# Bias of a layer's outputs from VectorE to TensorE for four tiles, and a routing product one slot later

## The chip, the cores and the metric

The kernel runs on one core of a Trainium2 chip (trn2), in one launch. The metric is the device time in microseconds, the median of several executions. Engines are named as in the profile: PE is TensorE's matmul, PEld its weight load, DVE VectorE, ACT ScalarE, POOL GpSimd, SP SyncE, which issues most DMAs.

## The reference, cut to what matters

Input x has 2 batches of 2048 tokens of 256 values, float32 throughout. Everything is dense except the last layer, where each token uses one of 8 matrices:

```python
xn  = layernorm(layernorm(x)) * ln_gamma + ln_beta
q, k, v = heads(xn @ w_q.T), heads(xn @ w_k.T), heads(xn @ w_v.T)      # 4 heads of 64
sim = rmsnorm(q, q_gamma) * 64**-0.5 @ rmsnorm(k, k_gamma).T
y   = softmax(sim) @ v            # heads side by side again
y   = y @ w_o.T + b_o             # the bias that the change moves
x2  = x + layernorm(y)
h   = layernorm(x2)
e   = argmax(h @ gate_w.T)        # one of 8 experts for each token
out = x2 + layernorm(h + h @ expert_w[e].T)
```

## The kernel before

**Attention.** A batch has 16 tiles of 128 tokens. The attention of both batches is 256 steps `(b, qb, c, kc)`: four blocks of 512 queries, two pairs of heads, 16 tiles of keys. Two steps make a slot; there are 128 slots. Within a slot the instructions are issued in this order: the scores `s` of the next slot on PE (L1071) with their exponentials `p` on ACT (L1079); the additions of this slot's `p` to the row sums `acc` on DVE (L1112, L1114); then `between(now)`, which lets every waiting side job do its next piece; then the weighted sums `po` of this slot on PE (L1123). The order on every engine is fixed by this program order, and each engine works through its own queue in order. The scores have two PSUM buffers (`ps_s`), the exponentials five SBUF buffers (`p`), `po` one, and all side jobs share three PSUM buffers (`ps_m`). A `p` buffer is free when its addition on DVE and its weighted sum on PE are done.

**Side jobs** are Python generators in a queue with due slots; each `yield later(...)` or bare `yield` ends the piece of one slot. `project` makes the queries, keys and values. `block_sums` normalises a finished block. `tokens` takes one tile of 128 tokens through the output product `py` (L817), the bias `y` (L832), the first layernorm (`norm`, statistics on DVE at L387 and L389, the root on POOL at L383), the residual `x2` (L843) and the scores of the experts (L851).

**Routing.** Batch 0 is group A (16 tiles), the first 12 tiles of batch 1 are group B, and the last four tiles are computed against all experts after the attention. When the last tile of a group has its scores, `choose_all` (L585 to L593) picks the experts, and the generator `order` sorts the group by expert in three pieces: a rank product on PE (L603, L604) with some two dozen small DVE instructions (`count` to `pos`, L613 to L652); a second DVE piece (`sl` to `inrow`, L655 to L686); after one piece with nothing in it the source product `src` on PE (L696), 16 matmuls with 23 columns for A and 12 with 19 for B, and its copy on DVE (L703). Every float32 matmul is two records in the profile.

The last piece of `order` also queues what follows: one `places` job per tile of places (23 for A, 19 for B), which gathers the rows with an indirect DMA on POOL (L722), loads the expert's matrix through SP into a ring (L736), turns and multiplies them on PE (`pt_g` L744, `pe` L754) and normalises; and one `collect` job per tile of the group (16 for A), which gathers the result on POOL (L792), reads `x2` through SP (L800), adds on DVE (L804) and stores through SP (L808). One job starts per slot, beginning with the slot after the source product; the `collect` jobs of A so run up to the last slots of the attention. Their tile `fg` has two buffers: the gather of a `collect` waits for the store of the one two before. After the last slot, `finish()` orders what is left with planned costs: the places of B, the last four tiles, and the collects of B.

Of the kernel before, what the change touches and what calls it, by code (L numbers as in the profile page):

```python
# [9 lines left out]
F32 = mybir.dt.float32  # L10
# [3 lines left out]
ALU = mybir.AluOpType  # L14
# [11 lines left out]
def kernel(  # L26
# [16 lines left out]
    nc = tc.nc  # L43
    P = 128
# [4 lines left out]
    NCH = D // P  # L49
# [4 lines left out]
    QT4 = KB // P  # L54
# [121 lines left out]
    DG = D + E  # L176
# [4 lines left out]
    bias_o = const.tile([P, DG], F32, tag="bias_o", name="bias_o")  # L181
# [100 lines left out]
    def bounded_path():  # L282
# [23 lines left out]
        wk = path.enter_context(tc.tile_pool(name="wk", bufs=2))  # L306
# [8 lines left out]
        allones = route.tile([P, P], F32, tag="allones", name="allones")  # L315
# [37 lines left out]
        def ps_m(name):  # L353
            return psum.tile([P, KB], F32, tag="ps_m", name=name, bufs=3)
# [242 lines left out]
        def order(gr):  # L597
# [43 lines left out]
            start = small.tile([P, E], F32, tag="start", name=f"start{n}")  # L641
# [49 lines left out]
                )  # L691
            yield
            yield
            ps = ps_m(f"src{n}")
            for t in range(T):
                nc.tensor.matmul(  # L696
# [3 lines left out]
                    start=(t == 0),  # L700
                    stop=(t == T - 1),
# [109 lines left out]
        def tokens(bt, qb, j, oTs, gr):  # L811


            tt = bt.b * NT + qb * QT4 + j
            py = ps_m(f"py{tt}")[:, :DG]
            for c, oT in enumerate(oTs):
                nc.tensor.matmul(  # L817
                    py,
                    oT[:, bass.ts(j, P)],
                    woT[:, c, :],  # L820
                    start=(c == 0),
                    stop=(c == NCH - 1),
                )
            yield then("DVE", 1.1)
            if gr:
                y = wk.tile([P, DG], F32, tag="y", name=f"y{tt}", bufs=3)
                xr = wk.tile([P, D], F32, tag="xr", name=f"xr{tt}")
            else:
                kept = wk.tile([P, HP, KB], F32, tag="p", name=f"kept{tt}", bufs=5)
                x2n, last = kept[:, 0, :D], kept[:, 0, D:]  # L830
                y, xr = kept[:, 1, KB - DG :], last
            nc.vector.tensor_tensor(y, py, bias_o, ALU.add)  # L832
            nc.sync.dma_start(out=xr, in_=x_f[tt * P : (tt + 1) * P, :])
            if gr:
                away = gr.away[:, tt - gr.first : tt - gr.first + 1]
# [18 lines left out]
            if not gr:  # L854
                pick = choose(small, score, tt)
            else:
                gr.met += 1
                if gr.met == gr.T:
                    choose_all(gr)
                    queue.append((now + 1 if gr is groups[0] else now, order(gr)))  # L860
                    queue.sort(key=lambda q: q[0])
# [22 lines left out]
            f = None  # L884
            EB = KB // D
            for e in range(E):
                if e % (HP * EB) == 0:
# [3 lines left out]
                    for r in range(HP):  # L891
                        for c in range(NCH):
# [6 lines left out]
                                start=(c == 0),  # L899
                                stop=(c == NCH - 1),  # L900
# [12 lines left out]
                f = z  # L913
# [61 lines left out]
        def finish():  # L975
# [3 lines left out]
            while queue or running:  # L979
                best = None  # L980
                for rank, g in enumerate(running + [g for _, g in queue]):
                    step = nexts.get(g) or opening.get(g) or Next("", 0.0)
                    if any(have[k] < step.take.count(k) for k in step.take):
                        continue
                    since = gates[g]() if g in gates else 0.0
                    if since is None:
                        continue
                    at = max(ready.get(g, 0.0), since, clear.get(step.engine, 0.0))
                    order = order_of.get(g, 0) if step.order < 0 else step.order
                    key = (at, order, rank)  # L990
                    if best is None or key < best[0]:
                        best = key, g, step
                (at, *_), g, step = best
                if g not in running:
                    queue[:] = [q for q in queue if q[1] is not g]
                    running.append(g)
                gates.pop(g, None)
                opening.pop(g, None)
                clock = end = at + step.cost
                clear[step.engine] = end if step.engine else 0.0  # L1000
                for k in step.take:
                    have[k] -= 1
                step = next(g, running)
                settle(g, step)
                if step is running:
                    running.remove(g)
                else:
                    ready[g] = end + (step.wait if step else 0.0)
# [4 lines left out]
        def opens(g, step, order, gate=None):  # L1013


            opening[g], order_of[g] = step, order
            if gate:
                gates[g] = gate
            return g
# [12 lines left out]
        groups = []  # L1032
# [107 lines left out]
        for g in range(len(steps) // PAIR):  # L1140
# [14 lines left out]
            b, qb, c, kc = steps[mine[-1]]  # L1155
            if kc == NT - 1:
                oT = wk.tile([P, KB], F32, tag="oT", name=f"oT{g}", bufs=4)
                nc.scalar.copy(oT, po)
                w = opens(block_sums(g, acc, oT), Next("PE", 1.0, take="m"), 0)
                queue.append((now, w))  # L1160
                oTs.append(oT)
                if c == NCH - 1:
                    tt = b * NT + qb * QT4
                    gr = next((g for g in groups if g.first <= tt < g.first + g.T), None)
                    last = gr and tt + QT4 == gr.first + gr.T
                    gap = (2 if gr is groups[0] else 1) if last else 4 if following else 1
                    for j in range(QT4):
                        w = tokens(batches[b], qb, j, oTs, gr)
                        end = (len(steps) // PAIR - 1, j)
                        opens(w, Next("PE", 0.5, take="m"), 0, lambda end=end: normed.get(end))  # L1170
                        queue.append((now + 2 + gap * j, w))
                    oTs = []
                queue.sort(key=lambda q: q[0])
# [381 lines left out]
```

## Time and profile before

| | |
|---|---|
| median of 3 executions | 804.57 us (802.62 to 805.9) |
| profiled execution: its own time | 796.33 us |
| profiled execution: span | 794.6 us |
| PE busy | 760.0 us, 96% |
| DVE busy | 607.9 us, 77% |
| ACT busy | 459.6 us, 58% |
| POOL busy | 323.9 us, 41% |
| mean granted TensorE clock | 0.982 |
| source product A starts | 460.6 us |
| rank product B starts | 678.4 us |
| last scores of the attention start | 711.4 us |

The profiled execution lies 8.2 us below the median of the others; 1.7 us of its own time lie around the span. Times such as "460.6 us" count from the start of the span. Lines of a timeline read: start, duration, engine, line, operation, output and inputs, count, and in brackets the idle time of the engine just before and what ended it.

### The profile page before, as it was taken

To read this page: it belongs to the slowest core of one execution; us is meant where nothing else is said; L and a number is where in the kernel's file an instruction comes from. 1 tells how busy PE (TensorE), PEld (TensorE's weight loads), DVE (VectorE), ACT (ScalarE), POOL (GpSimd) and SP (SyncE) were. 2 spreads that over 40 slices of the span, in tenths; PEclk is the share of its full clock that TensorE was granted. 3 is DMA by queue.
4 is the path that set the end of the run, shared out by engine and by line. 5 is a ranking of instruction groups with operands and counts; after the bars stand their busy time and mean duration, and the time that the engine had idled before them with its cause. 6 is when DMAs were issued, how large, how long until landed. Compare 5 with 4: busy or idle time off the path is not lost.

```text
span 794.6 us, 10249 instructions
## 1 busy us (share of the span) xinstructions
PE 760.0 (96%) x3169; PEld 320.3 (40%) x3169; DVE 607.9 (77%) x1239; ACT 459.6 (58%) x725; POOL 323.9 (41%) x349
## 2 busy tenths in 40 slices
PE   7999999999999999999999989999999999898794
PEld 5555433433343334333333343444444333335452
DVE  3666567598886877887888986777786889996767
ACT  3766765656565566556556525566656555445861
POOL 4644311133342523432325121757663455335324
PEclk9999999999999999999999979999999999899998
DMA  4100121210110000000221040443421243358336
GB/s 129 55 27 26 41 80 40 67 34 19 35 34 7 21 21 20 21 21 20 73 81 47 27 132 14 127 132 110 112 66 34 80 120 99 124 155 255 90 114 188
DMA packets 48149, 57.57 MB, mean 72 GB/s; under 512 B 5868, under 2 KB 39416, under 8 KB 48088
## 3 DMA queue, kind: packets, MB, share of 16 engines
q1 hardware_dynamic: 41528, 44.65, 17.8%
q0 software_dynamic: 3568, 9.32, 4.7%
q10 hardware_dynamic: 2992, 2.88, 1.3%
q8 instruction: 27, 0.44, 0.3%
q14 instruction: 34, 0.28, 0.1%
HBM read 37.69 MB, written 19.14 MB: 72 GB/s over the span
## 4 chain that ended last, share of the span: by engine, by line
PE 85%; DVE 8%; ACT 3%; issue 2%; POOL 2%; DMA 1%; POOLq 0%; DVEq 0%; ACTq 0%
PE s L1071 28%; PE po L1123 27%; PE pqk L464 7%; PE pv L473 4%; PE py L817 3%; PE peA L754 3%; PE pe L893 2%; PE pt_qk L501 2%; PE sm L1087 2%; DVE acc L1114 2%; PE pt_x L451 1%; PE peB L754 1%; DVE acc L1099 1%; PE srcA L696 1%; PE pt_gA L744 1%
## 5 line engine op out<-in xcount | busy, mean ns | idle before, releaser
L1079 ACT ACTIVATE p<-s,nbound 128x1024 f32<-128x1024 f32 x256 | 271.4, 1110 | 232.2 <-PE s L1071 224.5
L1114 DVE TENSOR_TENSOR acc<-acc,p 128x1024 f32<-128x1024 f32 x224 | 273.8, 1222 | 37.0 <-ACT p L1079 25.5
L1071 PE MATMUL s<-QT,KT 64*128 64x512 f32 x1024 | 256.5, 619 | 0.4 <-ACT p L1079 0.4
L1123 PE MATMUL po<-p,V 128*64 128x512 f32 x1024 | 251.6, 613 | 0.0
L1071 PEld LDWEIGHTS s<-QT,KT 64*128 64x128 f32 x1024 | 89.0, 188 | 164.6 <-issue 96.1
L1123 PEld LDWEIGHTS po<-p,V 128*64 128x64 f32 x1024 | 64.1, 137 | 129.8 <-issue 127.3
L383 POOL TENSOR_TENSOR rs_z<-rs_t,mhalf 128x1 f32<-128x1 f32 x28 | 36.8, 1316 | 123.3 <-DVE rs_t L382 123.2
L383 POOL TENSOR_TENSOR rn<-rs_t,mhalf 128x8 f32<-128x8 f32 x32 | 58.6, 1831 | 69.3 <-DVE rs_t L382 69.3
L464 PE MATMUL pqk<-wqkT,xnT 128*128 128x512 f32 x128 | 62.4, 611 | 0.6 <-ACT xnT L455 0.6
L383 POOL TENSOR_TENSOR roots<-rs_t,mhalf 128x1 f32<-128x1 f32 x32 | 23.9, 747 | 93.3 <-DVE rs_t L382 93.1
L1099 DVE RECIPROCAL acc<-acc 128x128 f32<-128x128 f32 x60 | 56.7, 945 | 0.0
L383 POOL TENSOR_TENSOR rs_y<-rs_t,mhalf 128x1 f32<-128x1 f32 x28 | 33.7, 1204 | 35.4 <-DVE rs_t L382 32.8
L832 DVE TENSOR_TENSOR y<-py,bias_o 128x264 f32<-128x264 f32 x28 | 12.0, 430 | 41.8 <-PE py L817 41.8
L722 POOL DMA_INDIRECT rows<-x2nA,srcA x23 | 28.9, 1257 | 30.1 <-DMA ring<-weTd 24.7
L817 PE MATMUL py<-woT,oT 128*128 128x264 f32 x128 | 35.7, 402 | 3.6 <-ACT xTB L749 2.3
L792 POOL DMA_INDIRECT fgA<-fnA,posA x16 | 18.2, 1136 | 44.8 <-DMA out_dram<-fgA 10.3
L473 PE MATMUL pv<-wvT,xnT 128*128 128x264 f32 x128 | 33.7, 386 | 0.0
L487 DVE TENSOR_REDUCE ss<-sq 128x8 f32<-128x512 f32 x32 | 21.8, 680 | 14.9 <-ACT sq L484 14.9
L473 PEld LDWEIGHTS pv<-wvT,xnT 128*128 128x128 f32 x128 | 24.5, 191 | 17.8 <-issue 10.4
L817 PEld LDWEIGHTS py<-woT,oT 128*128 128x128 f32 x128 | 22.0, 189 | 18.9 <-issue 12.1
L464 PEld LDWEIGHTS pqk<-wqkT,xnT 128*128 128x128 f32 x128 | 22.3, 195 | 17.7 <-issue 16.6
L481 ACT COPY qk<-pqk 128x512 f32<-128x512 f32 x32 | 18.7, 585 | 17.6 <-PE pqk L464 17.4
(270 smaller groups left out, 882.1 us busy)
## 6 DMA issues: line engine op xcount, KB each, us to landing
ring<-weTd SPq DMA_DIRECT2D x34, 256.0 KB, 2.9
x<-in_L_attn_x_dram SPq DMA_DIRECT2D x8, 512.0 KB, 3.9
xr<-in_L_attn_x_dram SPq DMA_DIRECT2D x28, 128.0 KB, 2.3
fnA<-fA SPq DMA_DIRECT2D x23, 128.0 KB, 2.5
we_raw<-in_L_ffn_expert_w_dram ACTq DMA_DIRECT2D x8, 256.0 KB, 2.7
weTd<-weT SPq DMA_DIRECT2D x8, 256.0 KB, 2.0
x2A<-x SPq DMA_DIRECT2D x16, 128.0 KB, 1.7
fgA<-x2A SPq DMA_DIRECT2D x16, 128.0 KB, 2.0
```

The lines of the kernel that those rows point to most:

```text
L383: nc.gpsimd.tensor_tensor(dst, t[:, :n], mhalf[:, :n], ALU.pow)
L464: nc.tensor.matmul(pqk, xnT[:, c, :], wqkT[:, c, :, :].rearrange("p a d -> p (a d)"), start=(c == 0), stop=(c == NCH - 1),)
L473: nc.tensor.matmul(pv[:, :DG], xnT[:, c, :], wvT[:, c, :], start=(c == 0), stop=(c == NCH - 1),)
L487: nc.vector.tensor_reduce(ss, sq.rearrange("p (g d) -> p g d", d=DH), AX.X, ALU.add)
L722: nc.gpsimd.indirect_dma_start(out=xg, out_offset=None, in_=gr.x2n[:, :], in_offset=bass.IndirectOffsetOnAxis(ap=gr.src[:, j : j + 1], axi ...
L754: nc.tensor.matmul(pe, xT[:, c, :], w[:, c, :], start=(c == 0), stop=(c == NCH - 1))
L817: nc.tensor.matmul(py, oT[:, bass.ts(j, P)], woT[:, c, :], start=(c == 0), stop=(c == NCH - 1),)
L1071: nc.tensor.matmul(s[:, r, :], bt.KT[rows, c, bass.ts(kc, P)], bt.QT[qb][rows, c, :], start=True, stop=True,)
L1079: nc.scalar.activation(p, s, AF.Exp, bias=nbound)
L1099: nc.vector.reciprocal(acc[:, 0, cols], share[:, cols])
L1114: nc.vector.tensor_tensor(acc, acc, p, ALU.add)
L1123: nc.tensor.matmul(po[r * DH : (r + 1) * DH, :], batches[b].V[:, kc, h * DH : (h + 1) * DH], p[:, r, :], start=(kc == 0), stop=(kc == NT - 1),
```

## The change

For group B's last four tiles (24 to 27 of all 32) `tokens` no longer adds the bias on DVE. PE adds it with a third matmul in the same PSUM group: a row of ones (one row, 128 columns) times the bias row (264 columns). The tile `y` is then the PSUM tile `py` itself, and the statistics, the residual and the experts' scores of those tiles read PSUM. In `order`, group A gets one more empty piece ahead of its source product.

```diff
@@ order
             yield
             yield
+            if gr is groups[0]:
+                yield
             ps = ps_m(f"src{n}")
@@ tokens
             tt = bt.b * NT + qb * QT4 + j
+            stays = gr is groups[1] and tt >= gr.first + gr.T - QT4
             py = ps_m(f"py{tt}")[:, :DG]
             for c, oT in enumerate(oTs):
                 nc.tensor.matmul(
                     py,
                     oT[:, bass.ts(j, P)],
                     woT[:, c, :],
                     start=(c == 0),
-                    stop=(c == NCH - 1),
-                )
+                    stop=(c == NCH - 1) and not stays,
+                )
+            if stays:
+                nc.tensor.matmul(py, allones[0:1, :], bias_o[0:1, :], start=False, stop=True)
             yield then("DVE", 1.1)
             if gr:
-                y = wk.tile([P, DG], F32, tag="y", name=f"y{tt}", bufs=3)
+                y = py if stays else wk.tile([P, DG], F32, tag="y", name=f"y{tt}", bufs=3)
...
-            nc.vector.tensor_tensor(y, py, bias_o, ALU.add)
+            if not stays:
+                nc.vector.tensor_tensor(y, py, bias_o, ALU.add)
```

## The prediction

> **What bounds the kernel now.** I read the page first, then PE's list of waits, then the timeline around the two waits, then the stretches of the granted clock.
>
> ```profile
> PE 760.0 (96%) x3169; PEld 320.3 (40%) x3169; DVE 607.9 (77%) x1239; ACT 459.6 (58%) x725; POOL 323.9 (41%) x349
> ...
> PEclk9999999999999999999999979999999999899998
> ```
>
> PE is busy all the time, so a microsecond of PE is a microsecond of the kernel, except where PE waits. The clock row has one 7: there the clock was withdrawn. Of PE's waits (engine, line, whom it waited for, us), two are long, and they are the two places of the change:
>
> ```profile
> PE rankB L603 <- DVE picksB L593: 4.4, 1, 4.4
> PE srcA L696 <- DVE inrowA L686: 4.0, 1, 4.0
> ```
>
> Between 480 and 650 us the list has nothing: PE alone sets the pace there, and whatever moves by a slot on another engine is covered. Around source product A:
>
> ```profile
> 454.64 1.99 PE L1071 MATMUL s<-QT,KT 64*128 64x512 f32 x8
> 460.61 5.91 PE L696 MATMUL srcA<-idsA,inrowA 128*128 128x23 f32 x32 [3.98 <-DVE inrowA L686]
> 466.44 3.68 PE L1123 MATMUL po<-p,V 128*64 128x512 f32 x8
> ...
> 455.84 1.11 ACT L1079 ACTIVATE p<-s,nbound 128x1024 f32<-128x1024 f32 x1 [0.50 <-PE s L1071]
> 463.59 1.11 ACT L1079 ACTIVATE p<-s,nbound 128x1024 f32<-128x1024 f32 x1 [6.64 <-DVE acc L1114]
> ```
>
> PE waits until 460.61; then `po` takes 3.68 where 1.94 is usual. The two ACT rows matter most: of the two exponentials of one slot the second starts 7.75 us after the first, because all five `p` buffers are taken until DVE, behind with the routing, does an addition at 462.28. Stretches of 3.41 us (PE, PEld, DVE, ACT, POOL busy, granted clock, DMA):
>
> ```profile
> 455.04:458.45 3.41, 1.58 (x8) 0.38 (x4) 3.27 (x8) 1.42 (x2) 0.00 (x0) 1.00 0.00 0
> 458.45:461.86 3.41, 1.25 (x12) 1.25 (x12) 3.31 (x9) 0.00 (x0) 0.00 (x0) 1.00 0.55 158
> 461.86:465.28 3.42, 3.42 (x19) 3.42 (x18) 3.32 (x4) 1.11 (x1) 0.00 (x0) 0.50 0.77 227
> 465.28:468.69 3.41, 3.41 (x12) 1.88 (x14) 3.26 (x6) 0.00 (x0) 0.00 (x0) 0.50 0.75 229
> 468.69:472.10 3.41, 3.41 (x10) 1.02 (x8) 2.34 (x2) 0.00 (x0) 2.94 (x2) 0.50 0.14 32
> 472.10:475.52 3.42, 3.42 (x18) 1.04 (x16) 2.09 (x2) 2.12 (x2) 2.71 (x3) 1.00 0.32 86
> ```
>
> The clock falls to half after a stretch with little wide work (none in the second row, whose 1.25 us are the 23-column product) and stays up after one with 1.58 us of it. It comes back only after a stretch full of 512-column work (fifth row); the third, full of the narrow product, did not count. So source product A costs its wait of 4.0 us and about 5 us of half clock (5.91 + 3.68 + 2.98 us where about 3.7, 1.9 and 1.9 would do; 3.7 is B's rate, 2.85 us for 24 records).
>
> **The change, part 1: the source product one slot later.** Nothing is added; PE's order becomes `po`, `s`, `src` instead of `src`, `po`, `s`. Up to the copy of `src` DVE's order is the old one, so the addition at 462.28 and the exponential at 463.59 stay where they are. PE, step by step, from 456.55 (end of the scores begun at 454.64): `po` 1.87, to 458.4 (its exponentials ended at 455.3). Of the next `s`, the first half finds its PSUM buffer free (exponential of 455.84): 0.96, to 459.4. The second half needs the buffer that the exponential of 463.59 reads, so PE waits to 464.75: 5.4 us in place of 4.0. The stretch that ended at 461.86 then holds 0.9 us of wide work, and the one from 693.97, with 3.41 less 2.53 of narrow product, or 0.88 us, was followed by half clock, so the clock falls:
>
> ```profile
> 693.97:697.38 3.41, 3.41 (x28) 2.85 (x29) 3.38 (x5) 1.19 (x2) 0.00 (x0) 1.00 0.63 208
> 697.38:700.80 3.42, 3.42 (x10) 1.08 (x8) 3.28 (x7) 0.00 (x0) 1.24 (x1) 0.50 0.61 176
> ```
>
> At half clock (3.61 over 1.87 is a factor 1.93) the second half takes 1.85, to 466.6. Then all of the source product: before, 12 of its records took 1.25 us at full clock and the other 20 took 4.65, or 0.23 each; 32 of these are 7.2 us, to 473.8. `po` 3.6, to 477.4. The first stretch full of wide work ends at 478.9, and the rest of `s` is done at 480.0. Before, the same work was done at 476.8. That is **+3.2 us**. In this execution the fall came as late as the wait allows (461.86; a stretch ending between 458.6 and 462.0 could do it), which flatters the kernel before by some 0.7 us on average, so I take +2.8, bounds +1 and +5.
>
> The Trainium skill speaks against the half-clock part of this sum: "TensorE: Matmul & The Clock Gate", Part 1, says that whatever is issued in the first 3.4 us or so runs at half clock and all after it at full. By that rule the second half of `s` and seven records of `src` are slow, the rest takes 2.8, `po` 1.9, `s` 1.9, and the work ends near 475, a gain of 2, with which the whole sum would be +0.8. This trace shows 10.2 us at half clock with the source product inside, so I follow the rows.
>
> Everything hanging on `src` moves too. On DVE the copy moves behind two more additions (2.5 us, waited for by nobody but the gathers). On POOL the 23 gathers of A, on SP their matrix loads, on PE the 23 turns and products start one slot later; the first turn before came at 485, over 10 us after its gather, so nothing new is waited for. PE's sum is the same and DVE has gaps of 1 to 3 us in many slots there: nothing. The 16 collects also move one slot, and their last one lands where it matters (part 3).
>
> **Part 2: the bias.** DVE loses 4 instructions of 0.43. PE gains 8 records; the trace has no one-row matmul, so I take the row of `py`: 1.09 us for 4, 0.27 each, 2.2 in all (bounds 0.9 by the 0.11 of a narrow record, and 2.2). PE has room: it waits 4.4 us for DVE just after. Reading PSUM instead of SBUF: residual-like rows are 0.484 (`f` from PSUM) and 0.480 (`x` from SBUF), so nothing. The skill ("Perfetto Trace Analysis", Optimizing Scalar/DVE Operations) gives DVE some 65 ns more per access to PSUM, 0.8 us for the 12 instructions; by it the rank product below would come 0.2 later and the sum be 0.2 higher. The rows decide. `py` keeps its `ps_m` buffer a slot longer, but in those slots only `py` uses `ps_m`, and two of three are taken at most.
>
> DVE then: for tile 24 it waits for PE anyway (0.38 before `y`) and gains nothing. Tiles 25 to 27 save 0.43 each, 1.3. But `x` of tiles 26 and 27 already waits 0.45 each for POOL, whose chain (store of `fgA` landing, gather, two roots) takes 6.1 to 6.6 us from one `fgA` addition to `x`; DVE reaching it sooner waits longer. Rank product B comes 0.9 earlier, at 677.5. PE, 2.2 later, waits 1.4 instead of 4.4; a stretch then keeps 2 us of wide work and the clock stays up, which before cost `rank`, `po` and `s` 2.5 us. PE gains 3.4, and 1.6 more if the half clock after source product B does not come back. DVE, busy without a gap from 676 to 708, gains the 0.9.
>
> **Part 3: what comes after.** PE would reach the turn of B's first gather at 708 to 710 instead of 713.3. The rows on whose account it will wait:
>
> ```profile
> 705.65 1.12 POOL L792 DMA_INDIRECT fgA<-fnA,posA  x1 [5.25 <-DMA out_dram<-fgA]
> 707.08 1.03 POOL L722 DMA_INDIRECT rows<-x2nB,srcB  x1 [0.30 <-PE po L1123]
> ...
> 701.29 0.38 SPq L808 DMA_DIRECT2D out_dram<-fgA  x1
> 704.84 0.33 SPq L800 DMA_DIRECT2D fgA<-x2A  x1
> 707.48 3.10 SPq L808 DMA_DIRECT2D out_dram<-fgA  x2
> ...
> 713.29 0.44 PE L744 MATMUL pt_gB<-ident,rows 128*128 128x128 f32 x2
> ```
>
> POOL works in order, and B's gathers stand behind A's last collect, which waits for the store of the collect two before. That store, at 701.29, becomes the one that SP reaches at 707.48, or 706.6 with the 0.9. A store lands in 2.2 to 2.9, the last collect's gather starts near 709, B's first gather 1.43 after it, at 710.4 instead of 707.1, and lands 3.5 later: 713.9 at PE, +0.6. PE's gain is lost in a wait of 4 to 5.6 us in front of the turn, with a `po` behind it in the queue; then the clock is at half for one to two stretches of 3.4 us, half of which is lost: 1.7 to 3.4. With a chance of some 0.9 that the clock falls this is +2.2. Who waits: the copy of the last `po`, ACT's table load behind it (719.39) and the tail. Part 2 and 3 together **+2.8**, bounds -2.5 and +5.
>
> **Sum:** +2.8 +2.8 = **+5.6 us**: 796.3 becomes 801.9 in a profiled execution. The median of the runs lies 8.2 above that execution, for reasons that no row shows; I add the change to the median: **810.2**.
>
> **Rivals.**
> *Only the first loss.* The store lands sooner or SP is not behind, B's gather comes before PE, and DVE's 0.9 plus its slack before the table load (mean and variance ready at 717.74, load at 719.39: 1.65) come through, up to -2.5. Sum +0.3 to +3: 806. For it: stores have landed in 1.7. Against: SP's 704.84 waited for a landing too, so the chain is tight.
> *Faster: PE does not stop for a `p` buffer.* If the slot's second exponential ends before 459.4 instead of 464.7, PE goes from `po` through all of `s` into a source product whose inputs are ready at 460.6 to 462.4; the wait of 4.0 and some 3 of the 5 us of half clock go, -7. With part 3 as above that is 800.4, without its loss 797.6. Against: the ACT row names DVE's addition, and DVE's order up to it is unchanged.
> *Worse.* Half clock for two full stretches at both places, and a gather slowed by the matrix loads: 814.
>
> **How the numbers follow.** The forecast has 0.58, only the first loss 0.22, faster 0.09, worse 0.11. About 0.5% (4.0 us: 800.6 and 808.6) is what a measurement of this kernel can tell from no change. The forecast's own range is 807 to 813, of which a sixth lies under 808.6; the first rival is all under it. Faster 0.09, same 0.32 (0.1 and 0.22), slower 0.59 (0.48 and 0.11). The range 804 to 814 leaves out the faster case and the upper half of the last.
>
> **What would show it.** Right: PE's list has a wait of `s` for ACT `p` of 5 us near 459 and no wait of `srcA`; `srcA` takes about 7 us, all at 0.5; a `po` after it above 3; `rankB` waits about 1.4 with the clock at 1.00; `pt_gB` waits for a POOL gather that starts after 709 + 3; the copy `y` is x24. Wrong: `srcA` in under 5 us, no wait of `s`, or `pt_gB` without a wait. The forecast is wrong as a whole if the attention's last scores end earlier than before by over 3 us and the tail follows them.

## The result, and the profile after

Beside the kernel before, which ran at 804.57 us again (802.62 to 805.9, 5 executions), the changed kernel takes **809.03 us** (808.08 to 810.36, 5 executions): +4.5 us, a ratio of 1.0062, 95% interval 1.0043 to 1.0081. In a later series it was 803.18 beside 797.34, +5.8 us, ratio 1.0073 (1.0047 to 1.0099). The kernel before stood at 804.6, 797.7, 797.3, 800.7 and 801.2 us in the five series of this study, so times are compared only within a series.

Engines and clock of the page after:

```profile
PE 766.0 (95%) x3177; PEld 322.8 (40%) x3177; DVE 606.7 (75%) x1235; ACT 459.9 (57%) x725; POOL 323.3 (40%) x349
PEclk9999999999999999999999969999999999999897
```

Eight records more on PE and 6 us more of busy time; DVE has four instructions less. The digit of the clock row where source product A lies fell from 7 to 6. PE's waits (engine, line, whom it waited for: us in total, times, longest):

```profile
PE s L1078 <- ACT p L1086: 5.6, 2, 5.2
PE pt_gB L746 <- DMA rows<-x2nB,srcB: 3.6, 1, 3.6
PE rankB L603 <- DVE picksB L593: 1.0, 1, 1.0
```

The wait of `srcA` is gone; `s` has a longer one in its place. The wait of `rankB` shrank from 4.4 to 1.0, and `pt_gB` has one that it did not have. The timeline around source product A:

```profile
457.47 1.13 PE L1078 MATMUL s<-QT,KT 64*128 64x512 f32 x4
463.81 2.08 PE L1078 MATMUL s<-QT,KT 64*128 64x512 f32 x4 [5.22 <-ACT p L1086]
465.82 7.02 PE L698 MATMUL srcA<-idsA,inrowA 128*128 128x23 f32 x32
472.77 3.68 PE L1130 MATMUL po<-p,V 128*64 128x512 f32 x8
...
462.65 1.11 ACT L1086 ACTIVATE p<-s,nbound 128x1024 f32<-128x1024 f32 x1 [6.67 <-DVE acc L1121]
```

Half of `s` goes through, the other half stops behind the exponential that waits for DVE's late addition. Then all of the source product and the `po` behind it run slowly (7.02 and 3.68 us). The same in stretches of 3.41 us (PE, PEld, DVE, ACT, POOL busy, granted clock, DMA share, GB/s):

```profile
456.77:460.18 3.41, 1.83 (x8) 0.30 (x4) 3.27 (x9) 0.00 (x0) 0.00 (x0) 1.00 0.38 109
460.18:463.60 3.42, 0.00 (x0) 0.00 (x0) 3.32 (x5) 0.95 (x1) 0.00 (x0) 1.00 0.74 240
463.60:467.01 3.41, 3.20 (x10) 1.69 (x10) 3.27 (x5) 1.98 (x3) 0.00 (x0) 0.51 0.77 235
467.01:470.42 3.41, 3.41 (x18) 3.41 (x17) 2.98 (x3) 0.40 (x1) 0.00 (x0) 0.50 0.08 30
470.42:473.84 3.42, 3.42 (x16) 2.75 (x17) 0.96 (x2) 0.00 (x0) 0.49 (x1) 0.50 0.01 2
473.84:477.25 3.41, 3.41 (x10) 0.82 (x8) 1.58 (x2) 0.00 (x0) 2.80 (x3) 0.50 0.16 38
477.25:480.66 3.41, 3.41 (x18) 0.93 (x14) 0.52 (x1) 2.12 (x2) 0.67 (x1) 0.99 0.29 77
```

After the empty second stretch the clock is at half for four stretches, 13.7 us, where it was 10.2 before. In these four stretches PE is busy for 3.20 us or more of 3.41; a busy PE at 0.50 and one at 1.00 look alike in the busy column. PE's timeline at the bias and the rank product B:

```profile
670.21 0.71 PE L829 MATMUL py<-bias_o,allones 1*128 1x264 f32 x2
...
679.48 0.46 PE L603 MATMUL rankB<-picksB,before 128*128 128x96 f32 x2 [0.99 <-DVE picksB L593]
```

And the timeline of POOL, SP and PE at B's first gather (SPq rows are DMAs that SP issues):

```profile
711.38 1.00 POOL L794 DMA_INDIRECT fgA<-fnA,posA  x1 [3.41 <-DVE acc L1121]
712.68 1.00 POOL L724 DMA_INDIRECT rows<-x2nB,srcB  x1 [0.30 <-issue]
...
708.84 0.34 SPq L810 DMA_DIRECT2D out_dram<-fgA  x1
...
715.80 0.44 PE L746 MATMUL pt_gB<-ident,rows 128*128 128x128 f32 x2 [3.59 <-DMA rows<-x2nB,srcB]
716.17 3.63 PE L1130 MATMUL po<-p,V 128*64 128x512 f32 x8
```

The gather stands behind A's last collect as foretold. The profile names an addition of DVE as what ended that collect's wait of 3.41; it was the store issued at 708.84, as e5 and e6 below show. PE stops for the gather, and the `po` behind it runs at half clock (3.63 for 1.94).

**A ruler for the traces.** To compare executions without their tails, the table takes the start of the four-record product `sm` (the sums of a finished attention block) on PE near 436, 481, 642, 685 and 721 us. Each kernel's start less that of the first profiled execution of before, both set to zero at 436: what was lost (+) or gained (-) up to there. The measure carries the chance of the first execution: differences of 1 us between executions of one kernel occur (before, second). Up to 481 lies source product A (part 1), from 642 to 685 the bias and rank product B (part 2), from 685 to 721 B's first gather (part 3). "Half clock" is the length of the stretch at source product A.

| kernel | 481 | 642 | 685 | 721 | half clock, us | time in its series |
|---|---|---|---|---|---|---|
| before, first execution | 0 | 0 | 0 | 0 | 10.2 | |
| before, second (e4) | -0.13 | -0.13 | -1.00 | -1.00 | 10.2 | +0.1 |
| after, first | +2.93 | +2.93 | -0.46 | +5.16 | 13.7 | +4.5 |
| after, second (e5) | +3.38 | +3.38 | -0.02 | +5.82 | 17.1 | +5.8 |
| e1 late product alone | +3.46 | +3.46 | +3.60 | +6.35 | 17.1 | +7.3 |
| e2 bias alone | +1.09 | +1.09 | -2.29 | -2.08 | 13.7 | -0.9 |
| e3 after, collects earlier | +3.22 | +3.22 | +10.74 | +10.74 | 17.1 | +13.1 |
| e6 after, three `fg` | +2.27 | +2.27 | -2.18 | -1.68 | 13.7 | +1.3 |
| e7 bias, filler | -3.57 | -3.57 | -6.95 | -6.75 | 0 | -3.3 |
| e8 after, additions on POOL | -2.28 | -2.29 | -5.68 | -1.49 | 6.8 | +2.3 |
| e9 e6 and e8 together | -2.26 | -2.26 | -6.71 | -6.08 | 6.8 | -3.3 |
| e10 bias, three `fg` | +0.01 | 0.00 | -4.44 | -5.66 | 10.2 | -4.5 |
| e11 e7, filler in the tail | -3.54 | -3.54 | -6.91 | -6.65 | 0 | -3.3 |
| e12 e7, three `fg` | +1.36 | +1.35 | -3.09 | -4.25 | 10.2 | -6.9 |

### The profile page after: what moved, and what is told of

Read it like the earlier page. It is cut to its first block, busy times and chain, and to the rows that moved or that the text cites. A ratio compares the mean times of both kernels' runs of the same rounds, so it can differ in the third digit from the quotient of the medians.

```text
span 806.3 us, 10261 instructions
## 1 busy us (share of the span) xinstructions
PE 766.0 (95%) x3177; PEld 322.8 (40%) x3177; DVE 606.7 (75%) x1235; ACT 459.9 (57%) x725; POOL 323.3 (40%) x349
## 3 DMA queue, kind: packets, MB, share of 16 engines
q1 hardware_dynamic: 41528, 44.65, 17.1%
## 4 chain that ended last, share of the span: by engine, by line
PE 79%; DVE 11%; issue 3%; ACT 2%; DMA 2%; POOL 1%; another core or an unknown queue 0%; SPq 0%; DVEq 0%; POOLq 0%; ACTq 0%
PE s L1078 26%; PE po L1130 25%; PE pqk L464 7%; PE pv L473 4%; PE py L821 3%; PE peA L756 3%; DVE acc L1121 2%; PE pt_qk L501 2%; PE pe L900 2%; PE sm L1094 2%; PE peB L756 1%; PE pt_x L451 1%; DVE acc L1106 1%; PE srcA L698 1%; DMA gk_all<-in_L_attn_k_gamma_dram 1%
## 5 line engine op out<-in xcount | busy, mean ns | idle before, releaser
L794 POOL DMA_INDIRECT fgA<-fnA,posA x16 | 19.0, 1185 | 47.8 <-DVE rs_t L382 13.7
L900 PE MATMUL pe<-weD,kept 128*128 128x512 f32 x64 | 29.6, 620 | 0.0
L495 DVE TENSOR_TENSOR qk<-qk,rn 128x512 f32<-128x512 f32 x32 | 22.0, 687 | 9.1 <-POOL rn L383 6.9
```

The lines of the kernel that those rows point to most:

```text
L900: nc.tensor.matmul(pes[:, r].rearrange("p e d -> p (e d)"), xT[:, c, :], weD[:, c, e + r * EB : e + (r + 1) * EB, :].rearrange("p e d -> p ...
```

## The experiments

### Each half of the change alone (e1, e2)

e1 is the kernel before with only the extra piece; e2 is the kernel after without it:

```diff
+            if gr is groups[0]:
+                yield                 # e1: this alone; e2: all of the change but this
             ps = ps_m(f"src{n}")
```

> The kernel before with the source product of A one slot later and nothing else. Theory (half clock and the p buffer): PE waits 5 to 6 us in front of the second half of an s for ACT's p near 459, srcA takes about 7 us at 0.5; +2.9 us there. PE still stops at rankB for 4.4 us as before, so it reaches the turn of B's first gather no earlier than before, and the later gather costs 1 to 1.5 us there: in all +4 us, 808.6. Rival (the bias is what costs; the moved product is covered): within 0.5 us of before, 804.6, with a wait of s below 1 us.

Measured: 804.97 us beside 797.7, +7.3, ratio 1.0095 (1.0075 to 1.0116). PE's waits:

```profile
PE s L1073 <- ACT p L1081: 5.6, 2, 5.2
PE rankB L603 <- DVE picksB L593: 4.3, 1, 4.3
PE pt_gB L746 <- DMA rows<-x2nB,srcB: 2.7, 1, 2.7
```

Part 1 is as in the kernel after, +3.46 us in the ruler. The expectation, +4 us in all, missed at `pt_gB`, by a factor of two (2.75 us from 685 to 721 for 1 to 1.5): in this execution the half clock after source product B did not come, PE gained 1.5 us there and gave them back in front of the gather. So the gather sets this point with or without the bias.

> The kernel before with the bias of the last four tiles on TensorE and nothing else. Theory: rankB waits 1 to 1.5 us instead of 4.4, the clock stays at 1.00 there, PE is 3.4 us ahead; A's collects are in their old slots, so B's first gather starts near 706.5 and the wait at pt_gB is under 1 us: -2.5 us, 802.1. Rival (the bias is what costs, PE's eight records and DVE's reads of PSUM): +1 to +3 us, 806 to 808. Rival (PE's gain is lost at B's first gather even with the collects in their old slots): pt_gB waits 3 us or more, within 1 us of before.

Measured: 796.78 us beside 797.7, -0.9; by the ratio 0.998 (0.9966 to 0.9995) 0.4 to 2.7 us faster. The wait of `rankB` is 1.0, and the timeline has the gather in time:

```profile
705.79 1.00 POOL L722 DMA_INDIRECT rows<-x2nB,srcB  x1 [0.30 <-issue]
...
709.60 0.44 PE L744 MATMUL pt_gB<-ident,rows 128*128 128x128 f32 x2
```

The two rivals that blamed the bias fall: from 642 to 685 it brings 3.38 us, as much as in the kernel after. The expectation was -2.5 us, and only 0.9 arrives. The profiled execution shows where single executions lose it: a fourth stretch of half clock at source product A (+1.09), and half clock in the tail, as e4 has it below. Against e4 it is 1.1 us ahead at 721 us and 0.7 at the end. Whether that explains the median of 22 executions was not shown. Together the two single changes come to about +6 us, which is what both make: the whole loss comes from the late product.

### The collects back in their old slots (e3)

```diff
-                queue.append((at + 5, g))
+                queue.append((at + (4 if gr is groups[0] and t >= 8 else 5), g))
```

> The kernel after with the last eight collects of A queued one slot earlier, as in the kernel before; the source product stays late, the bias on TensorE. Theory: B's first gather starts about 3 us earlier than in the kernel after, the wait of 3.6 us at pt_gB falls under 1 us and the half-clock stretch behind it goes: 4 to 5 us under the kernel after, 804.5. Rival (the collects are not what holds the gather back): the wait stays at 3 us or more and the time at 809.

Measured: 810.8 us beside 797.7, +13.1. The wait at `pt_gB` did go, but another came in PE's list of waits:

```profile
PE rankB L603 <- DVE picksB L593: 9.9, 1, 9.9
```

The timeline of POOL and DVE before it:

```profile
669.72 1.02 POOL L794 DMA_INDIRECT fgA<-fnA,posA  x1 [4.52 <-DMA out_dram<-fgA]
670.77 0.58 POOL L383 TENSOR_TENSOR rs_y<-rs_t,mhalf 128x1 f32<-128x1 f32 x1
...
671.67 0.54 POOL L383 TENSOR_TENSOR rs_z<-rs_t,mhalf 128x1 f32<-128x1 f32 x1
...
672.25 0.48 DVE L850 SCALAR_TENSOR_TENSOR x<-py,rs_z,xr 128x256 f32<-128x256 f32 x1 [5.09 <-POOL rs_z L383]
```

The collect stood on POOL ahead of the roots `rs_z` that tiles of the last block need, and waited there 4.52 us for a store to land; DVE's `x` waited 5.09 for the root. By the edit the eighth and ninth collects share a slot, which two buffers may not carry; that this set off the delay is argued, not tested. So this run says nothing on the price of the late gather, but it shows the chain that sets both places: store of a collect, the gather two collects on, and whatever is queued behind it on POOL.

### The kernel before, again (e4)

> The kernel before, unchanged, for a second profiled execution and the spread of a difference of zero. Theory: the 8.2 us between the first profiled execution (796.3) and the median (804.6) lie in the tail after 725 us, as stretches of half clock that the first execution did not have; up to 721 the two executions agree within 1 us. Rival: the difference is spread over the whole span.

Measured: 797.76 us beside 797.7, ratio 1.0003 (0.9988 to 1.0018). Its clock row:

```profile
PEclk9999999999999999999999979999999999899698
```

The 6 near the end is the theory's stretch: 3.4 us at half clock from 725.4 and 13.7 from 739.1, which the first execution did not have. From 721 us to the last expert product it loses 4.7 us on the first. But that is the difference of two single executions, and not of the medians: the first profiled execution (796.33) lies only 1.4 us under this series' median of 797.7. The other 6.9 of the 8.2 us are the level of the first series, 804.57; what sets that level was not found.

### The kernel after, again, and three buffers for the collects (e5, e6)

> The kernel after, unchanged, beside before in this series, for a second profiled execution. Theory: +4.5 to +6 us over before; the same three places as in the first profiled execution: s waits 5.2 us for ACT's p, rankB about 1, pt_gB 3 to 4. Rival (what differed was the tail of single executions and not these places): the waits differ and the difference is under 3 us.

Measured: 803.18 us, +5.8. The waits recur: `s` 5.2, `pt_gB` 3.9, `rankB` 1.0. Here the profile itself puts the wait of A's last collect down to the store:

```profile
712.07 1.00 POOL L794 DMA_INDIRECT fgA<-fnA,posA  x1 [3.42 <-DMA out_dram<-fgA]
```

A standstill of PE, ACT and DVE near 737 to 739 us and other late losses of the first execution after (its span is 11.7 longer than that of before, though it lags only 5.16 at 721) do not recur: they are not the change's. The first execution of after is also the only trace from the first series, so these losses may be what its level consists of; that was not shown.

e6 is the kernel after with this edit, paid for with one buffer less for `y` and for `xr`:

```diff
-                z = wk.tile([P, 2 * D], F32, tag="fg", name=f"fg{n}")
+                z = wk.tile([P, 2 * D], F32, tag="fg", name=f"fg{n}", bufs=3)
...
-                y = py if stays else wk.tile([P, DG], F32, tag="y", name=f"y{tt}", bufs=3)
-                xr = wk.tile([P, D], F32, tag="xr", name=f"xr{tt}")
+                y = py if stays else wk.tile([P, DG], F32, tag="y", name=f"y{tt}", bufs=2)
+                xr = wk.tile([P, D], F32, tag="xr", name=f"xr{tt}", bufs=1)
```

> The kernel after with three fg buffers for A's collects instead of two (paid for by two y buffers instead of three and one xr instead of two). Theory: A's last collect no longer waits for the store of the collect two before it, so B's first gather, which stands behind it on POOL, starts 3 us or more earlier; the wait at pt_gB falls under 1 us and the half clock behind it goes: 3.5 to 5 us under the kernel after. Rival (POOL is late for another reason than that store, say DVE's srcB or the matrix loads): pt_gB still waits 3 us, within 1.5 us of the kernel after.

Measured: 798.64 us beside 803.18, 4.5 under the kernel after. The timeline of B's first gather and of the turn that waited for it:

```profile
706.92 1.00 POOL L724 DMA_INDIRECT rows<-x2nB,srcB  x1 [0.30 <-PE po L1130]
...
710.06 0.44 PE L746 MATMUL pt_gB<-ident,rows 128*128 128x128 f32 x2 [0.43 <-DMA rows<-x2nB,srcB]
```

From 685 to 721 it loses 0.5 us instead of 5.8, and the gather starts 5.1 to 5.7 us earlier than in the two executions of after (all set to zero at 436). Part 3 is the store that a collect's buffer waits for.

### Three buffers where the gather is not late (e10)

The same edit on the kernel with the bias alone, as a control.

> The kernel with the bias alone and three fg buffers. Theory (the third buffer helps only where the last collect is late): with the source product in its old slot pt_gB does not wait for its gather in any case, so within 1 us of the kernel with the bias alone: 0.9 to 1.6 us under before. Rival (a third buffer is worth 4 us wherever collects run, and part 3 was not the cause): 4 to 6 us under before.

Measured: 796.21 us beside 800.69, -4.5, ratio 0.9943 (0.9922 to 0.9963): outside the theory, inside the rival's figure. The ruler shows more: the third buffer also helps at `rankB`, since POOL is no longer held there by a collect (642 to 685: -4.44 instead of -3.38; DVE's waits of 0.9 and 0.4 for `rs_z` are gone), and in this execution no half clock followed source product B. From 685 to 721 it gives 1.4 us, against 5.3 in the kernel after. So by the traces some 1 us of e6's gain is not the late gather, and most of the rest is. By the times alone this stays open: from e2 to e10 the third buffer brings 3.6 us, from e5 to e6 4.5, each uncertain by about 2.

### Part 1: the buffer and the clock (e8, e7)

e8 is the kernel after, with the two additions behind the second routing piece moved to the idle POOL:

```diff
+            if gr is groups[0]:
+                relief.update(now + k for k in (2,))
...
+            eng = nc.gpsimd if now in relief else nc.vector
...
-                nc.vector.tensor_tensor(acc, acc, p, ALU.add)
+                eng.tensor_tensor(acc, acc, p, ALU.add)
```

> The kernel after, with the two additions that stand behind A's second routing piece (DVE, 1.27 us each, begun at 462.28 in the trace of before) done by POOL, which is idle from 444 to 468. Theory (the p buffer that DVE's late addition holds is what PE waits for in part 1): the additions end by 461 at the latest, the wait of s for ACT's p falls from 5.2 to under 2 us, the source product starts near 461 to 462 at full or half clock; 3 to 6 us under the kernel after. Rival (PE would wait as long for inrow or for the clock in any case): the wait moves to srcA, and the time stays within 1.5 us of the kernel after.

Measured: 799.68 us beside 803.18, 3.5 under the kernel after. The timeline by engine:

```profile
453.89 4.95 POOL L1125 TENSOR_TENSOR acc<-acc,p 128x1024 f32<-128x1024 f32 x2 [11.45 <-DVE acc L1125]
...
454.64 1.75 DVE L1110 TENSOR_TENSOR oT<-oT,acc 128x128 f32<-128x128 f32 x1
457.02 1.85 DVE L665 CAST expA<-expfA 128x23 int32<-128x23 f32 x1
...
456.28 1.11 ACT L1089 ACTIVATE p<-s,nbound 128x1024 f32<-128x1024 f32 x1 [1.08 <-POOL acc L1125]
...
456.70 1.99 PE L1081 MATMUL s<-QT,KT 64*128 64x512 f32 x8
462.02 5.75 PE L700 MATMUL srcA<-idsA,inrowA 128*128 128x23 f32 x32 [3.34 <-DVE inrowA L688]
```

The second exponential of the slot starts at 456.28, where it started at 462.65 in the kernel after, and all of `s` goes through without a wait: the late addition was the cause. What is left is a wait of 3.34 for DVE's `inrowA` and 6.8 us of half clock. The rival is right in that the wait moves to `srcA`; but 3.1 us of DVE's lateness there are the price of POOL's additions (the rows of `oT` and `expA`; see the last section). At 481 the kernel is 5.2 to 5.7 us ahead of the two executions after.

e7 is the kernel with the bias alone and filler on PE around A's source product:

```diff
+            over = ps_m(f"hold{n}") if gr is groups[0] else None
+            fill = woT[:, 0, :]
+            for _ in range(6 if gr is groups[0] else 0):
+                nc.tensor.matmul(over[:, :DG], ident, fill, start=True, stop=True)
             for t in range(T):
+                if gr is groups[0] and t and t % 4 == 0:
+                    nc.tensor.matmul(over[:, :DG], ident, fill, start=True, stop=True)
```

> The kernel with the bias alone (source product in its old slot), with filler on TensorE: six matmuls of 264 columns into an unused PSUM tile ahead of A's source product, in the wait of 4.0 us, and one more after each quarter of it. Each is two records of 0.27 us: 3.3 us in the wait and 1.6 us on PE's path. The filler's result is not used. Theory (half clock comes from too little wide work): the clock stays at 1.00 through the product; srcA with its filler takes 5.3 us, po and s behind it 1.9 each instead of 3.7 and 3.0: 3 to 4 us under the kernel with the bias alone, -4 us against before. Rival (the narrow records are slow whatever the clock): 1.6 us over the kernel with the bias alone.

Measured: 794.03 us beside 797.34, -3.3, ratio 0.9964 (0.9938 to 0.999). PE's timeline:

```profile
455.51 2.94 PE L698 MATMUL holdA<-woT,ident 128*128 128x264 f32 x12
459.55 1.07 PE L702 MATMUL srcA<-idsA,inrowA 128*128 128x23 f32 x8 [1.10 <-DVE inrowA L686]
...
464.57 1.94 PE L1134 MATMUL po<-p,V 128*64 128x512 f32 x8
```

Work was added and time fell: the product with its filler ends at 464.6, and `po` takes 1.94 again. At 481 it stands 3.4 to 3.6 us ahead of the two executions of before and of e10, and 4.7 ahead of e2 with its fourth stretch. That is what holding the clock is worth with the product in its old slot, after the filler's own cost; the narrow records by themselves are not slow (8 in 0.97 us). By the medians, over two series, some 2.4 of it arrives (-3.3 less e2's -0.9), under the 3 to 4 expected. The filler also ends most of PE's idle time, so this run alone doesn't say that width counts. The prediction's row from 693.97 does: PE was busy there for all of 3.41 us, with 0.9 of it wide, and half clock followed.

### Both reliefs, the tail's clock, and the best of all (e9, e11, e12)

> The kernel after with both reliefs: three fg buffers and the two additions on POOL. Theory (the loss of the kernel after is the sum of two separate things, part 1 at the p buffer and part 3 at B's first gather, and what is left is the gain at rankB): the two reliefs add, -4.5 and -3.5 us against the kernel after, 795 where before is 797.4, so 2 us under before. Rival (the reliefs overlap, since one wait takes up what the other gives): no better than the better of the two, 798 to 799.

Measured: 797.35 us beside 800.69, -3.3, ratio 0.9958 (0.9935 to 0.9981). The ruler shows both reliefs at work: up to 481 it stands where e8 does (-2.26 and -2.28), and from 685 to 721 it loses 0.6 us, as e6 does (0.5), where e8 alone loses 4.2. The two losses are separate. By the times, it lies 9 us under the kernel after of the series before, each set against its own before, uncertain by about 3.

e11 adds one filler matmul behind each turn of a B tile in the tail:

```diff
+            if not attending:
+                nc.tensor.matmul(pt[:, D:], ident, woT[:, 0, :D], start=True, stop=True)
             yield then("ACT", 0.4)
```

> The kernel with the bias alone and the filler around A's source product, and one more filler matmul of 256 columns behind each turn of a B tile in the tail, some 17 of 0.5 us each, into unused columns. The filler's result is not used. Theory (the tail's stretches of half clock, 10 to 17 us in most executions, come from too little wide work and cost half of their length): the clock holds in the tail; 3 to 5 us of half clock saved against up to 8 us of filler, a good part of it in PE's waits: between -3 and +3 us against the run without the tail's filler, which was 3.3 us under before. Rival (the tail's half clock has another cause): the clock falls as before and the time is 3 to 8 us longer than without.

Measured: 797.37 us beside 800.69, -3.3, as e7 without it. The clock row holds from 692.6 to 784.8:

```profile
PEclk9999999999999999999999999999999999999997
```

The mean granted clock of its 11 executions is 0.984 to 0.993 (median 0.988), of e7's 12 it is 0.976 to 0.994 (0.983). So wide work holds the clock in the tail too, and there the filler costs what it brings.

e12 is e7 with three `fg` buffers.

> The kernel with the bias on TensorE for the last four tiles, the source product of A in its old slot with the filler around it, and three fg buffers. Theory (the filler acts at A's source product, the third buffer at rankB and at B's source product, so the gains add): -3.3 and -3 us, 5 to 7 us under before. Rival (both gains end in the same limit of the tail, which starts no earlier): no better than the better of the two, -3.5 to -4.5 us.

Measured: **794.33 us** (792.0 to 799.05) beside 801.21: -6.9, ratio **0.9911** (0.9887 to 0.9936), the fastest kernel here against its own before. Its own time is that of e7 (794.03, where before stood at 797.34), so how much of the -6.9 is the level of its series is open, and so is whether the two gains add. Its profiled execution was its slowest, and there the filler did not hold the clock (columns as in the stretches above):

```profile
457.50:460.90 3.40, 2.27 (x17) 1.80 (x15) 3.37 (x7) 0.00 (x0) 0.00 (x0) 1.00 0.74 184
460.90:464.30 3.40, 3.40 (x16) 3.19 (x15) 3.26 (x4) 1.11 (x1) 0.00 (x0) 0.50 0.77 243
```

PE was busy with filler for 1.09 us of the first of these stretches, and half clock followed; in e7 and e11, where the grid of stretches fell otherwise, the poorest had 1.39 and 1.48 and the clock stayed. More filler in the wait may hold it more often; that was not tried.

## Why the prediction was right

Its forecast was +5.6 us, 810.2; measured +4.5, 809.0, with +5.8 in the second series. By the ruler, the kernel after lies 5.2 and 5.8 us behind the first execution of before at 721, which is where its sum ends (6.2 and 6.8 behind the second, e4). The mechanism was right at all three places: the new wait of `s`, the shorter one of `rankB`, the gather behind the store. That the number is so close is in part luck, as the terms show.

**Part 1** was +3.2 in the step by step and +2.8 as taken. The five late executions that were left as they were there (both of after, e1, e3, e6) have +2.3 to +3.5, mean 3.05; the four early ones (both of before, e2, e10) -0.1 to +1.1, mean 0.24; difference **2.8**. The wait was 5.2 for 5.4 foretold, the product 7.02 for 7.2, all at half clock. The working has two slips, which nearly cancel: 32 records of 0.23 us are 7.4 and not 7.2, and for the lucky grid it names 0.7 us and takes off 0.4. The correction was right in kind, 0.24 as measured: one of the early executions had a fourth stretch of half clock.

**Where the skill spoke against it**, the Trainium skill's "TensorE: Matmul & The Clock Gate", Part 1, would have let the clock return within some 3.4 us, a sum of +0.8. The clock stayed at half for 13.7 and 17.1 us, with PE busy for most of it; e7 shows that wide work ahead of and among the same narrow records keeps it. So being busy is not enough here; what counts is wide work. Following the row was the step that decided.

**Part 2.** PE's gain from 642 to 685 was to be 3.4 (0.9 from DVE, 2.5 from the clock) and is 3.39, 3.40 and, with the bias alone, 3.38, all against the execution that the forecast was read from. There the half clock at rank product B lasted two stretches, in e4 one, and against e4 the gain is only 2.5: so the exact match is luck. The terms: rank product B started at 677.5 in before's time, as foretold; the eight records took 2.54 us, not 2.2 (the lag grows from 1.98 to 4.52 over the four tiles): 0.32 each, not 0.27; why is not shown. So `rankB` waited 1.0, not 1.4. Reading PSUM costs DVE nothing, as taken from the rows (`x` takes 481 ns from either); groups of the trace after (busy us, mean ns of one):

```profile
L387 DVE BATCH_NORM_STATS2 st_z<-y 128x6 f32<-128x256 f32 x24 | 10.3, 428 | 0.8
...
L387 DVE BATCH_NORM_STATS2 st_z<-py 128x6 f32<-128x256 f32 x4 | 1.7, 424 | 1.0 <-PE py L829 1.0
```

**Part 3** was to lose what part 2 gained and more: +0.6 at the gather and 2.2 by the clock, +2.8 for parts 2 and 3. Measured +2.2 and +2.4. The gather was foretold for 710.4 in before's time and started 712.68 less the lag of 1.98, 710.7; PE's turn 713.9, measured 713.8. The wait was 3.6 to 3.9 us, just under the 4 foretold for the case that the half clock after source product B comes back, as it did; the 0.3 us more that the bias cost PE make up the difference. The half clock behind it was one stretch, the shorter of the two cases.

**What it did not see.** It tied part 3 to PE's coming early after part 2. e1 shows that the late gather costs 2.75 us without the bias too. The sum was right for the pair, and its split by cause was not: all of the loss belongs to the late product, and the bias alone is a small gain. And of the 8.2 us between the profiled execution and the median, which it left open, 6.9 are the level of the first series, whose cause stays open, and 1.4 lie within the spread of a series, to which half clock in the tail adds up to 4.7.

**The rivals.** "Only the first loss" fell at the gather, "worse" at one stretch instead of two. "Faster" needed the exponential to end by 459.4; e8 gave it that (459.1 in before's time), and came 5.2 to 5.7 us ahead of after at 481, less than the rival's 7 since PE then stopped for `inrowA`.

## What to carry to other kernels

Putting a step later takes its wait away and hands it to whatever is next in that engine's order: look for the buffer that the next instruction needs, and follow the moved step's last DMA to the end of every queue it passes. On TensorE, read each wait with the clock behind it: a wait followed by narrow work can cost its length and several microseconds of half clock more, and here filler in the wait gained some 3.5 us up to 481 without shortening anything. Where the buffer of a gather and its store paces a queue, try one more buffer first: here it gained 4.5 us, and the one other schedule that was tried (e3) lost 7.

## What the hardware showed that was not expected

- In e8 an addition of 128x1024 takes POOL 2.4 to 2.5 us and DVE 1.27, and DVE suffers meanwhile: its product `oT` took 1.75 instead of 0.29 and the cast `expA` 1.85 instead of 0.18, each ending within 0.15 us behind the end of one of POOL's two additions (456.25 and 458.84), while a reciprocal and a reduction beside them ran as usual. The Trainium skill's "Advanced Engine Details and Errata", GPSIMD Details, has POOL share an interface with DVE that only some of DVE's instructions need; this agrees.
- How much wide work holds the clock has no sharp bound in these traces. Counted as the busy time of PE's records of 256 columns or more in a stretch of 3.41 us, less than 1.0 us always lost it and more than 1.7 always kept it; between them both happened. The first row below is e3, where 1.20 us of `s` and the end of a `po` was followed by half clock; in the second, of e1, `po` was busy for 1.08 us beside the narrow product, and the clock stayed at 1.00 (columns as in the stretches above).

```profile
458.70:462.11 3.41, 1.20 (x6) 0.30 (x4) 3.31 (x9) 0.00 (x0) 0.00 (x0) 1.00 0.53 150
...
696.23:699.64 3.41, 3.41 (x28) 2.78 (x29) 3.38 (x5) 0.98 (x1) 0.00 (x0) 1.00 0.60 186
```

- Nor does the clock return only after a stretch full of 512-column work, as the rows of the first trace suggested: in e9 it returned after a stretch in which PE was busy for 2.87 us, with nothing wider than 264 columns (720.30 to 723.72).
- Executions of one kernel differ by up to 1% without any change: 803.13 and 794.66 us are the same kernel, e10, at a mean granted clock of 0.974 and 0.987. Between the two traces of before most of the difference lies in the tail (4.7 us after 721, and 1.0 the other way up to there). Single profiles can mislead by as much as this change was worth.
